# Five changes to the schedule of a network with state-space scans: places of table-switching pieces, of sums, of a copy, the share of products, and the order of directions

## The chip, the cores and the metric

The kernel runs on one core of one Trainium2 chip. The metric is the device time of one execution in microseconds (us). Most sets of executions of one kernel agree within about 0.3%; the widest, of the kernel with only the products changed, spans 0.6% (9307 to 9360). All runs told here were in the fast state, and all gave correct results. Blocks, rounds and waits are read from the one profiled run of each kernel, so differences of blocks of a few us are not clear of noise.

Engines are named as the profile names them: PE (matmuls), DVE (vector), ACT (scalar functions), POOL (GpSimd), SP (issues DMA).

## The reference, cut to what matters

Four images of 56 x 56 = 3136 tokens with 96 channels go through four layers. Layers 0 and 1 are selective scans in four directions (along rows, rows reversed, columns, columns reversed), with 192 inner channels and 16 states:

```python
def step(h, inp):
    da_t, db_t, x_t, c_t = inp
    h = da_t * h + db_t * x_t[..., None]
    y_t = jnp.einsum('bds,bs->bd', h, c_t)
    return (h, y_t)
# ... d_a = exp(softplus(dt) * a), and before and after the scans:
# norms, projections with silu, gelu, a 3x3 depthwise convolution
```

Layers 2 and 3 are a linear attention and a feed-forward block in low precision. Everything except the scans is small beside them.

## The kernel before: the parts that the change and the argument touch

The scans of one layer and image are a *block*; there are 8 (blocks 0 to 3 are layer 0, 4 to 7 layer 1). A block has 4 directions of 7 *chunks* (448 tokens), a chunk has 8 *rounds*, r = 0 to 7, which are two halves of the channels (e) by four groups of states (q). The kernel fixes the order of instructions on PE, ACT, DVE and POOL by hand:

```python
        def decay(n, g):               # ACT: da = exp(dt * a)
            ...
        def begin(n):
            b = self.spread_b(ch, q)                              # PE
            v = sp.tile([128, NG, CS + 2], F32, name="v", bufs=3)
            ahead = NQ * e + q not in (OWN_TAIL if ch.l and ch.i else OWN)
            if ahead:                                             # POOL's product
                nc.gpsimd.tensor_tensor(v[:, 2, TOKENS], ch.du[e][:, 2], ch.cb[q][:, 1], ALU.mult)
            return b, v, ahead
        ...
        for n, (ch, e, q) in enumerate(rounds):
            for g in range(2 if ahead else 3):                    # DVE's products
                nc.vector.tensor_tensor(v[:, g, TOKENS], ch.du[e][:, g], b, ALU.mult)
            nxt = begin(n + 1)
            self.prepare(ch, nexts.get(ch), r)   # next chunk: r == 2 is softplus on ACT
            yield "C", n, r                      # a slot for pieces of the rest
            if late is not None and late[2] == 0 and n > 1:
                self.keep_sums(*rounds[n - 2])   # ACT stores y (r = 1 and 5)
            for g in range(NG):
                if g == 2:
                    yield "F", n, r              # a second slot
                nc.vector.tensor_tensor_scan(...)                 # DVE
                ...
                decay(n + 1, g)                  # ACT, may start when scan g is done
                if g == 1:
                    carried(n + 1, nxt[1])       # ACT: state of the chunk before
            nc.gpsimd.tensor_tensor(hc, v, c)                     # POOL
            if late is not None:
                self.add_up(*late)               # PE: y += four * hc, one round late
            late = (ch, e, q, hc)
```

`da`, `b` and `y` each have one buffer per use in PSUM, `v` has three, `hc` two. The "rest" (loading and projections beside block 0, the middle layer beside blocks 1 to 4, fusion and attention of images 0 to 2 beside blocks 5 to 7) is cut into pieces that run in the slots. Fusion and attention of image 3 run alone after the last scan, three parts in flight and two PSUM banks for them.

## Time and profile before

| | before |
|---|---|
| time, median of three runs | 9285 us |
| first scan starts at | 121 us |
| block 0 / blocks 1 to 4, mean / blocks 5 to 7, mean | 1015 / 1083 / 1110 us |
| last scan to end | 507 us |
| mean length of rounds r = 2 in these three groups | 5.18 / 5.80 / 6.15 us |

(The prediction's 6.17 for the last of these leaves one chunk out.) Lengths of blocks and rounds in this document are read from the start times of the scans: a round lasts from its first scan to the next round's first. The prediction shows the busy times. To them belongs the list of who waited for whom (columns: engine and line, what it waited for, us in total, times, longest):

```profile
ACT Y L663 <- PE y L658: 623.0, 340, 10.0
...
DVE v L626 <- ACT v L599: 298.2, 269, 6.7
...
DVE v L612 <- PE b L535: 275.0, 185, 11.0
...
POOL hc L636 <- PE y L651: 195.5, 143, 9.6
```

The first line is `keep_sums`: ACT stood 623 us for the sums that it had to store. That is a large number on an engine that is 65% busy; whether it costs anything depends on what stands behind it in ACT's queue, which is the thread of this study. The second line is the scan that waits for the copy of the carried state, the third a product that waits for `b`, the fourth POOL, which can't overwrite `hc` until the sums have read it.

### The profile page before, as it was taken

The page shows a single profiled execution, that of the slowest core. Times are in us where ns is not written, and L with a number is a line of the kernel's source. Part 1 is how long each engine was busy: PE and PEld are TensorE (multiplying, and loading weights), DVE is VectorE, ACT ScalarE, POOL GpSimd, SP SyncE. Part 2 cuts the span into 40 slices and gives each one's busy share as a digit, 9 for nine tenths or more (in the row PEclk, how much of TensorE's full clock was granted, in tenths as well). Part 3 has the DMA queues.
Part 4 walks back from the last instruction along what each step waited for, and adds up shares of the span by engine and source line. Part 5 has one row for each costly group of instructions (what it writes and reads, how often), then busy time and mean ns, then how long its engine had stood idle before and what let it go on. Part 6 is the DMA issues. An engine that isn't in the chain of part 4 may idle for free.

```text
span 9302.9 us, 112892 instructions
## 1 busy us (share of the span) xinstructions
PE 7648.6 (82%) x30134; PEld 2655.7 (29%) x30134; DVE 7967.6 (86%) x10251; ACT 6080.1 (65%) x12093; POOL 7416.2 (80%) x3872
## 2 busy tenths in 40 slices
PE   7788787787878778887878879888898879988786
PEld 3222122222222222221222223332332223332244
DVE  5999999988998989989898989999889998999711
ACT  5777677666776667666776656666666666666523
POOL 4889888878887888878887888888888888888711
PEclk8988899888888888888898889888898889988875
DMA  5777766656666676667666676656666666666411
GB/s 154 177 177 169 172 169 162 155 138 170 168 157 147 157 172 164 155 148 172 166 162 149 154 180 154 149 148 150 176 152 155 150 154 162 157 154 153 115 33 31
DMA packets 940551, 1415.81 MB, mean 152 GB/s; under 512 B 175042, under 2 KB 926148, under 8 KB 938276
## 3 DMA queue, kind: packets, MB, share of 16 engines
q1 hardware_dynamic: 939136, 1406.79, 62.0%
q8 instruction: 238, 3.90, 0.2%
q14 instruction: 405, 3.32, 0.1%
q10 hardware_dynamic: 772, 1.80, 0.1%
HBM read 1139.85 MB, written 268.14 MB: 151 GB/s over the span
## 4 chain that ended last, share of the span: by engine, by line
PE 31%; DVE 25%; issue 12%; ACT 12%; DMA 10%; POOL 6%; SPq 3%; DVEq 0%; POOLq 0%; ACTq 0%
DVE v L626 17%; DVE v L612 7%; PE b L535 6%; PE y L651 5%; PE ps L775 4%; POOL hc L636 4%; ACT da L584 4%; DMA cb<-cd 3%; PE y L658 3%; PE pp L401 2%; DMA du<-dd 2%; PE ps L693 2%; PE ps L701 1%; SPq L485 1%; ACT L584 1%
## 5 line engine op out<-in xcount | busy, mean ns | idle before, releaser
L636 POOL TENSOR_TENSOR hc<-v,cb 128x1344 f32<-128x1344 f32 x1792 | 5155.8, 2877 | 1033.1 <-DVE v L626 571.3
L626 DVE TENSOR_TENSOR_SCAN v<-da,v 128x449 f32<-128x449 f32 (+1 forms) x5376 | 5469.6, 1071 | 362.8 <-ACT v L599 298.2
L584 ACT ACTIVATE da<-dt,na 128x448 f32<-128x448 f32 x5376 | 3358.5, 634 | 1531.4 <-DVE v L626 1477.4
L535 PE MATMUL b<-cf,sel 128*128 128x448 f32 x3584 | 2062.6, 661 | 804.5 <-DVE v L612 794.2
L612 DVE TENSOR_TENSOR v<-du,b 128x448 f32<-128x448 f32 x4172 | 2332.5, 606 | 297.3 <-PE b L535 275.0
L651 PE MATMUL y<-hc,four 128*32 128x448 f32 x14336 | 1980.0, 628 | 424.5 <-POOL hc L636 396.2
L592 POOL TENSOR_TENSOR v<-du,cb 128x448 f32<-128x448 f32 x1204 | 1378.5, 1145 | 81.1 <-DMA cb<-cd 64.9
L535 PEld LDWEIGHTS b<-cf,sel 128*128 128x128 f32 x3584 | 636.8, 212 | 2406.3 <-DVE v L612 1793.5
L651 PEld LDWEIGHTS y<-hc,four 128*32 128x32 f32 x14336 | 298.6, 114 | 1856.3 <-POOL hc L636 1104.8
L697 POOL TENSOR_TENSOR rs<-rs,power 112x4 f32<-112x4 f32 x252 | 254.3, 1010 | 685.2 <-ACT rs L696 498.5
L663 ACT COPY Y<-y 96x448 f32<-96x448 f32 x448 | 340.7, 761 | 623.8 <-PE y L658 623.0
L401 PE MATMUL pp<-U,wd 96*128 96x448 f32 x896 | 645.0, 807 | 75.1 <-DMA wd<-in_wd_dram 69.8
L775 PE MATMUL ps<-win,dg 64*64 64x220 f32 (+11 forms) x2016 | 567.3, 479 | 31.2 <-ACT w L893 30.7
L468 POOL TENSOR_TENSOR duc<-dtc,U 96x448 f32<-96x448 f32 x448 | 562.7, 1256 | 11.6 <-ACT dtc L462 11.6
L658 PE MATMUL y<-Y,ident 96*96 96x448 f32 x672 | 546.6, 902 | 0.0
L584 ACT ACT_TABLE_LOAD x385 | 494.0, 1283 | 14.4 <-DMA dt<-dd 7.5
L630 ACT COPY carry<-v 128x3 f32<-128x3 f32 x1536 | 293.6, 191 | 127.2 <-DVE v L626 123.9
L693 PEld LDWEIGHTS ps<-avg,w 96*112 96x112 f32 (+1 forms) x2240 | 315.2, 208 | 126.1 <-issue 53.2
L775 PEld LDWEIGHTS ps<-win,dg 64*64 64x64 f32 (+2 forms) x2016 | 249.6, 166 | 324.0 <-issue 255.3
L701 PE MATMUL ps<-ident,rs 112*96 112x112 f32 x2016 | 301.6, 307 | 33.3 <-POOL rs L697 31.1
L701 PEld LDWEIGHTS ps<-ident,rs 112*96 112x96 f32 x2016 | 281.5, 203 | 156.4 <-issue 77.2
L693 PE MATMUL ps<-avg,w 96*112 96x1 f32 (+1 forms) x2240 | 308.5, 255 | 20.0 <-ACT w L680 5.1
(218 smaller groups left out, 5497.3 us busy)
## 6 DMA issues: line engine op xcount, KB each, us to landing
cb<-cd SPq DMA_DIRECT2D x3584, 112.0 KB, 4.0
dt<-dd SPq DMA_DIRECT2D x1792, 168.0 KB, 4.0
du<-dd SPq DMA_DIRECT2D x1792, 168.0 KB, 3.7
dd<-dtc SPq DMA_DIRECT2D x448, 168.0 KB, 2.0
dd<-duc SPq DMA_DIRECT2D x448, 168.0 KB, 2.0
U<-u SPq DMA_DIRECT2D x64, 294.0 KB, 6.9
y<-Y SPq DMA_DIRECT2D x16, 1176.0 KB, 6.7
z<-w SPq DMA_DIRECT2D x56, 224.0 KB, 2.4
```

The costliest lines, as they stand in the source:

```text
L401: self.nc.tensor.matmul(ch.ps.rearrange("p (a b) -> p a b", b=HS), ch.par.wx[:, e], self.in_order(self.U[e], ch.orient, ch.c * CS, CS), st ...
L535: self.nc.tensor.matmul(ps, self.sel[:, q], ch.cf, start=True, stop=True)
L584: nc.scalar.activation(da[g][:, TOKENS], ch.dt[e][:, g], AF.Exp, scale=ch.par.na[:, e, q, g : g + 1])
L592: nc.gpsimd.tensor_tensor(v[:, 2, TOKENS], ch.du[e][:, 2], ch.cb[q][:, 1], ALU.mult)
L612: nc.vector.tensor_tensor(v[:, g, TOKENS], ch.du[e][:, g], b, ALU.mult)
L626: nc.vector.tensor_tensor_scan(v[:, g, way], da[g][:, way], v[:, g, way], 0.0, ALU.mult, ALU.add)
L636: nc.gpsimd.tensor_tensor(hc, v[:, :, TOKENS], ch.cb[q][:, 0].unsqueeze(1).to_broadcast([128, NG, CS]), ALU.mult)
L651: nc.tensor.matmul(self.y[32 * n : 32 * n + 32], self.four, hc[:, g], start=q == 0 or n == 3, stop=n == 3,)
L658: nc.tensor.matmul(o, w, self.in_order(a, ch.orient, ch.c * CS, CS), start=False, stop=True)
L693: nc.tensor.matmul(ps[:NT, q : q + 1], sq[:, b], avg, start=n == 0, stop=n == len(terms) - 1)
L701: nc.tensor.matmul(ps[:, b], rs[:, q : q + 1].to_broadcast([NT, C]), self.ident[:NT, :NT], start=True, stop=True)
L775: self.nc.tensor.matmul(o[:, a - r0 : e - r0, x0:x1], diag[:, tap], win[:, a + dy - lo : e + dy - lo, x0 + dx : x1 + dx], start=n == 0, st ...
```

## The change

Its intent: keep ACT from holding up the scans (table-switching pieces only at r = 0, 4, 6; the copy of carried states first), keep PE's `b` from standing behind sums that wait for POOL (sums two rounds late), take one product in eight rounds from DVE, and shorten the end (start image 3's fusion early, more parts in flight). The diff, cut to its core:

```diff
-OWN = (3, 4, 5)
-OWN_TAIL = (4, 5)
+OWN = (3, 4)
+OWN_TAIL = (3,)
-TURNS = (150, 150, 150, 150, 150, 220, 220, 220)
+TURNS = (170, 180, 160, 160, 160, 220, 220, 220)
+SWITCH = (0, 4, 6)
-ORDER = ((0, 0), (0, 1), (1, 0), (1, 1))
+ORDER = (((0, 0), (0, 1), (1, 0), (1, 1)), ((0, 1), (1, 0), (1, 1), (0, 0)))
 ...                                   # in begin(n): the copy first
+            if ch.step:
+                at = CS + 1 if ch.rev else 0
+                nc.scalar.copy(v[:, :, at : at + 1], ch.par.carry[:, e, q].unsqueeze(2))
 ...                                   # in the loop: the sums
                 nxt = begin(n + 1)
+            ended = None
+            if len(late) == 2:
+                ended = late.pop(0)
+                self.add_up(*ended)
             self.prepare(ch, nexts.get(ch), r)
             yield "C", n, r
-            if late is not None and late[2] == 0 and n > 1:
-                self.keep_sums(*rounds[n - 2])
             for g in range(NG):
                 if g == 2:
+                    if ended and ended[2] == NQ - 1:
+                        self.keep_sums(*ended[:3])
                     yield "F", n, r
 ...
-                    if g == 1:
-                        carried(n + 1, nxt[1])
 ...
-            if late is not None:
-                self.add_up(*late)
-            late = (ch, e, q, hc)
+            late.append((ch, e, q, hc))
 ...                                   # in project(): a switching piece, split
-        yield "C1"
+        yield "T1"                     # T: only where r is in SWITCH, one per slot
         (two Silu)
+        yield "F1"
         (Identity, and the next matmul)
 ...                                   # gelu, conv silu: "C" becomes "T"
 ...                                   # the end
-    alone(net.tail(3))
+    alone(rest)                        # what is left of fuse(3)
+    net.late()                         # 24 work tiles, 8 PSUM banks, 6 in flight
+    alone(net.attend(3))
```

`TURNS` is, for each block, how many of its "C" slots may start pieces, spread over the block. With the last direction of layer 1 along rows, each chunk's sums are final when it ends; they are sent out chunk by chunk, and image 3's fusion may follow them.

More of the change, by code (lines that the diff above doesn't have):

```diff
@@ L1 @@
 from contextlib import ExitStack
-from itertools import chain
+from itertools import chain, cycle
 import numpy as np
@@ L36 @@
 RANK = (12, 6)
-NW = 13
+NW, LATE_NW = 13, 24
 NWIN = 3
-OWN = (3, 4, 5)
-OWN_TAIL = (4, 5)
+OWN = (3, 4)
+OWN_TAIL = (3,)
 FULL = 4 * NCS * NE * NQ - 13
-TURNS = (150, 150, 150, 150, 150, 220, 220, 220)
-BANKS = 2
-DEPTH = 3
-ORDER = ((0, 0), (0, 1), (1, 0), (1, 1))
+TURNS = (170, 180, 160, 160, 160, 220, 220, 220)
+SWITCH = (0, 4, 6)
+BANKS, LATE_BANKS = 2, 6
+DEPTH, LATE_DEPTH = 3, 6
+ORDER = (((0, 0), (0, 1), (1, 0), (1, 1)), ((0, 1), (1, 0), (1, 1), (0, 0)))
 WD = NE * 128 + C + NE + NE * NQ * NG
@@ L167, in __init__ @@
         self.dram = pool("dram", bufs=1, space=bass.MemoryType.DRAM)
+        self.nw, self.depth, self.banks, self.ring = NW, DEPTH, BANKS, None
         self.setup()
         self.dg = None
+        self.kept = (0, 0, 0)
         self.held = self.lend = 0
+        self.switch = True
         self.U = [self.big.tile([C, L], F32, name=f"U{e}") for e in range(NE)]
         self.Y = [self.big.tile([C, L], F32, name=f"Y{e}") for e in range(NE)]
-        self.sp = pool("scan", bufs=2)
         self.wp = pool("work", bufs=2)
+        self.scan_pool = ExitStack()
+        self.sp = self.scan_pool.enter_context(tc.tile_pool(name="scan", bufs=2))
+        self.pool = pool
         d = lambda name, *shape: [self.dram.tile(list(shape), F32, name=f"{name}{i}") for i in range(NB)]
@@ L177, in __init__, with late @@
         self.ud, self.zd, self.yd, self.md = d("u", DI, L), d("z", DI, L), d("y", DI, L), d("m", DI, L)
+    def late(self):
+        self.scan_pool.close()
+        self.wp = self.pool("late", bufs=2)
+        self.nw, self.depth, self.banks = LATE_NW, LATE_DEPTH, LATE_BANKS
+        tags = (("ps", BANKS), ("da0", 1), ("da1", 1), ("da2", 1), ("pp", 1), ("b", 1), ("y", 1))
+        self.ring = cycle([t for t in tags for _ in range(t[1])])
     def ps(self):
-        return self.psum.tile([128, 512], F32, tag="ps", name="ps", bufs=BANKS)
+        tag, bufs = next(self.ring) if self.ring else ("ps", BANKS)
+        return self.psum.tile([128, 512], F32, tag=tag, name=tag, bufs=bufs)
     def w(self, rows=128):
-        return self.wp.tile([128, CW], F32, tag="w", name="w", bufs=NW)[:rows]
+        return self.wp.tile([128, CW], F32, tag="w", name="w", bufs=self.nw)[:rows]
     def par(self, group, name):
@@ L549, in scans @@
             for i in range(NB):
-                for n, (orient, rev) in enumerate(ORDER):
+                for n, (orient, rev) in enumerate(ORDER[l]):
                     for step in range(NCS):
@@ L555, in scans @@
                         ch.c = NCS - 1 - step if rev else step
-                        ch.first = n == 0 and step == 0
+                        ch.n, ch.first = n, n == 0 and step == 0
                         ch.skip = n == 0
@@ L592, in begin @@
                 nc.gpsimd.tensor_tensor(v[:, 2, TOKENS], ch.du[e][:, 2], ch.cb[q][:, 1], ALU.mult)
+            if ch.step:
+                at = CS + 1 if ch.rev else 0
+                nc.scalar.copy(v[:, :, at : at + 1], ch.par.carry[:, e, q].unsqueeze(2))
             return b, v, ahead
-        def carried(n, v):
-            ch, e, q = rounds[n]
-            at = CS + 1 if ch.rev else 0
-            if ch.step:
-                nc.scalar.copy(v[:, :, at : at + 1], ch.par.carry[:, e, q].unsqueeze(2))
         nxt = begin(0)
@@ L603, in scans @@
             decay(0, g)
-        late = None
+        late = []
         for n, (ch, e, q) in enumerate(rounds):
@@ L632, in scans @@
                     decay(n + 1, g)
-                    if g == 1:
-                        carried(n + 1, nxt[1])
             hc = sp.tile([128, NG, CS], F32, name="hc")
             nc.gpsimd.tensor_tensor(hc, v[:, :, TOKENS], ch.cb[q][:, 0].unsqueeze(1).to_broadcast([128, NG, CS]), ALU.mult)
-            if late is not None:
-                self.add_up(*late)
-            late = (ch, e, q, hc)
-        self.add_up(*late)
+            late.append((ch, e, q, hc))
+        for ended in late:
+            self.add_up(*ended)
         self.keep_sums(ch, e, q)
@@ L663, in keep_sums @@
         self.nc.scalar.copy(y, self.y[:C].rearrange("p (a b) -> p a b", b=HS))
-        if ch.last:
-            self.nc.sync.dma_start(self.yd[ch.i][C * e : C * e + C], self.Y[e])
+        if ch.n < 3:
+            return
+        s = slice(ch.c * CS, (ch.c + 1) * CS) if ch.orient == 0 else slice(0, L)
+        if ch.orient == 0 or ch.last:
+            self.nc.sync.dma_start(self.yd[ch.i][C * e : C * e + C, s], self.Y[e][:, s])
+        if e == NE - 1:
+            self.kept = (ch.l, ch.i, ch.step + 1)
     def factor(self, *x):
@@ L789, in window, with overlap @@
         return t, lo
-    def overlap(self, part, n, depth):
+    def overlap(self, part, n, depth, ready=lambda c: True):
         live, c = [], 0
         while live or c < n:
-            if self.slot == "C" and c < n and len(live) < depth:
+            if self.slot == "C" and c < n and len(live) < depth and ready(c):
                 live.append([part(c), "C0", 0])
@@ L799, in overlap @@
                 new = int(g[1][1:])
-                if g[1][0] == self.slot and sum(h[2] for h in live) - g[2] + new <= BANKS - self.lend:
+                fits = self.switch if g[1][0] == "T" else g[1][0] == self.slot
+                if fits and sum(h[2] for h in live) - g[2] + new <= self.banks - self.lend:
+                    self.switch = self.switch and g[1][0] != "T"
                     g[1], g[2] = next(g[0], None), new
@@ L827, in part @@
             yield from self.project(0, i, xr, s)
-        yield from self.overlap(part, NCW, DEPTH)
+        yield from self.overlap(part, NCW, self.depth)
     def middle(self, i):
@@ L854, in part @@
             nc.tensor.matmul(ps[0], self.w1[:, :128], xr, start=True, stop=True)
-            yield "C0"
+            yield "T0"
             g.append(self.w())
@@ L861, in part @@
                 nc.tensor.matmul(ps[m], self.w1[:, m * 128 : (m + 1) * 128], xr, start=True, stop=True)
-            yield "C0"
+            yield "T0"
             for m in (1, 2):
@@ L874, in part @@
             yield from self.project(1, i, xr, s)
-        yield from self.overlap(part, NCW, DEPTH)
+        yield from self.overlap(part, NCW, self.depth)
         if self.dg is None:
@@ L890, in convolve @@
             yield from self.conv(dga, wa, lo, (ps, c * CR, CR))
-            yield "C1"
+            yield "T0"
             t = self.w()
             nc.scalar.activation(t, ps, AF.Silu, bias=par("c128", "1conv_ba"))
+            yield "C1"
             ps = self.ps()
@@ L897, in convolve @@
             nc.sync.dma_start(self.ud[i][:128, s], t)
-            yield "C0"
+            yield "T0"
             t = self.w(64)
@@ L915, in run, with fuse @@
         yield from self.overlap(whole, 1, 1)
-    def tail(self, i):
+    def fuse(self, i):
         nc = self.nc
@@ L989, in part, with attend @@
             yield from self.gram(0, i, c, x, s)
-        yield from self.overlap(part, NCW, DEPTH)
+        yield from self.overlap(part, NCW, self.depth, lambda c: self.kept >= (1, i, c + 1))
+    def attend(self, i):
+        nc = self.nc
+        par = self.par
         for n in range(2):
@@ L1013, in ffn @@
                 yield "C1"
-                xq = self.wp.tile([C, CW], F8, name="xq", bufs=DEPTH)
+                xq = self.wp.tile([C, CW], F8, name="xq", bufs=self.depth)
                 nc.vector.tensor_tensor(xq, xs, f, ALU.mult, saturate=False)
-                h = self.wp.tile([128, 3, CW], F16, name="h", bufs=2)
+                h = self.wp.tile([128, 3, CW], F16, name="h", bufs=self.depth - 1)
                 ps = self.ps()[:, :CW]
@@ L1031, in ffn @@
                 yield "C1"
-                hq = self.wp.tile([128, 3, CW], F8, name="hq", bufs=2)
+                hq = self.wp.tile([128, 3, CW], F8, name="hq", bufs=self.depth - 1)
                 nc.vector.tensor_copy(hq, h, saturate=False)
@@ L1037, in ffn @@
                 yield "F0"
-                y = self.wp.tile([C, CW], F16, name="yq", bufs=2)
+                y = self.wp.tile([C, CW], F16, name="yq", bufs=self.depth - 1)
                 nc.scalar.copy(y, ps)
@@ L1058, in ffn @@
                 )
-            yield from self.overlap(ffn, NCW, DEPTH)
+            yield from self.overlap(ffn, NCW, self.depth)
     def gram(self, n, i, c, x, s):
         nc = self.nc
-        xr = self.wp.tile([C + 1, CW], F32, name="xra", bufs=DEPTH)
+        xr = self.wp.tile([C + 1, CW], F32, name="xra", bufs=self.depth)
         nc.vector.memset(xr[C : C + 1], 1.0)
@@ L1132, in alone @@
     def alone(stage):
-        net.slot = "C"
+        net.slot, net.switch = "C", True
         for _ in stage:
             net.slot = "CF"[net.slot == "C"]
+            net.switch = net.slot == "C"
     alone(net.load(0))
@@ L1140, in tile_net @@
         [net.load(1), net.load(2), net.load(3)], [net.middle(0)], [net.middle(1)], [net.middle(2)], [net.middle(3)],
-        [net.tail(0)], [net.tail(1)], [net.tail(2)],
+        [net.fuse(0), net.attend(0)], [net.fuse(1), net.attend(1)], [net.fuse(2), net.attend(2), net.fuse(3)],
     ]
@@ L1148, in tile_net @@
             p, u = divmod(n, rounds)
-            net.slot, net.lend = slot, int(r == 1)
+            net.slot, net.lend, net.switch = slot, int(r == 1), slot == "C" and r in SWITCH
             if slot == "C" and u == 2 and p < 8:
@@ L1152, in tile_net @@
             if u < 2 or p == 8:
+                continue
+            if p == 7 and u > FULL:
+                next(rest, None)
                 continue
@@ L1158, in tile_net @@
                 next(rest, None)
-            if u == FULL and slot == "F":
+            if u == FULL and slot == "F" and p < 7:
                 for _ in rest:
                     net.slot = "CF"[net.slot == "C"]
-    alone(net.tail(3))
+                    net.switch = net.slot == "C"
+    net.lend = 0
+    alone(rest)
+    net.late()
+    alone(net.attend(3))
 def kernel(**inputs):
```

## The prediction

> **What bounds the kernel now.** The work is 1792 rounds: 8 blocks (2 layers x 4 images) of 224 rounds, a block being 28 chunks of 8 rounds (r = 0 to 7). Each round has three scans on DVE, three exponentials on ACT, one large product `hc` on POOL, a spread `b` and four sums `y` on PE. The rest of the network is cut into pieces that are slipped in between; that of image 3 runs alone at the end. I read the busy times and costliest groups of the page first.
>
> ```profile
> PE 7648.6 (82%) x30134; PEld 2655.7 (29%) x30134; DVE 7967.6 (86%) x10251; ACT 6080.1 (65%) x12093; POOL 7416.2 (80%) x3872
> ...
> L636 POOL TENSOR_TENSOR hc<-v,cb 128x1344 f32<-128x1344 f32 x1792 | 5155.8, 2877 | 1033.1 <-DVE v L626 571.3
> L626 DVE TENSOR_TENSOR_SCAN v<-da,v 128x449 f32<-128x449 f32 (+1 forms) x5376 | 5469.6, 1071 | 362.8 <-ACT v L599 298.2
> ...
> L612 DVE TENSOR_TENSOR v<-du,b 128x448 f32<-128x448 f32 x4172 | 2332.5, 606 | 297.3 <-PE b L535 275.0
> ...
> L592 POOL TENSOR_TENSOR v<-du,cb 128x448 f32<-128x448 f32 x1204 | 1378.5, 1145 | 81.1 <-DMA cb<-cd 64.9
> ```
>
> No engine is full, but DVE and POOL are close to it in the rounds. Two idle causes make up most of DVE's waiting: scans that wait for ACT's copy of the carried state (298 us) and products that wait for PE's `b` (275 us). Then the busy time by stretch (columns: length, PE, PEld, DVE, ACT, POOL busy with counts, granted clock, DMA share, GB/s): blocks 1 to 4, blocks 5 to 7, and the end in two halves.
>
> ```profile
> 1136.00:5467.00 4331.00, 3492.86 (x13440) 1095.81 (x13440) 3871.01 (x4928) 2988.15 (x5713) 3578.92 (x1811) 0.87 0.66 160
> 5467.00:8796.00 3329.00, 2880.77 (x11926) 1045.96 (x11926) 3051.26 (x3896) 2177.07 (x4589) 2875.74 (x1539) 0.89 0.63 155
> 8796.00:9028.00 232.00, 205.07 (x729) 104.77 (x725) 24.75 (x46) 44.94 (x91) 31.92 (x29) 0.78 0.12 35
> 9028.00:9303.00 275.00, 189.47 (x642) 118.12 (x642) 41.70 (x73) 90.69 (x183) 35.44 (x35) 0.51 0.11 32
> ```
>
> The last 507 us are image 3's fusion (232) and attention (275) with DVE and POOL almost idle. In the second half PE is busy 69% at a clock of 0.51.
>
> From the start times of the scans I took each round's length. Undisturbed rounds are 4.01 us with two products on DVE (three scans at 1.00, two products at about 0.5) and 4.55 with three. So a chunk can't be under 5 x 4.01 + 3 x 4.55 = 33.7 us in blocks 0 to 4 and 6 x 4.01 + 2 x 4.55 = 33.2 in 5 to 7. Measured blocks: 1015 (block 0), 1083 on average (1 to 4), 1110 (5 to 7); 28 chunks at the floor would be 944 and 928. Rounds with r = 2 are the worst: mean 5.18, 5.80, 6.17 us in the three groups. The timeline shows why:
>
> ```profile
> 3019.50 1.28 ACT L462 ACT_TABLE_LOAD   x1
> 3020.79 0.63 ACT L462 ACTIVATE dtc<-pp,wd 96x448 f32<-96x448 f32 x1
> ...
> 3022.50 0.63 ACT L462 ACTIVATE dtc<-pp,wd 96x448 f32<-96x448 f32 x1 [1.08 <-PE pp L449]
> 3023.15 1.28 ACT L584 ACT_TABLE_LOAD   x1
> ...
> 3024.45 1.19 ACT L584 ACTIVATE da<-dt,na 128x448 f32<-128x448 f32 x2
> ...
> 3025.58 0.18 ACT L599 COPY v<-carry 128x3 f32<-128x3 f32 x1
> ...
> 3025.79 3.06 DVE L626 TENSOR_TENSOR_SCAN v<-da,v 128x449 f32<-128x449 f32 x3 [1.92 <-ACT v L599]
> ```
>
> Softplus needs another table, twice switched, and the 0.18 us copy that the scan needs stands behind two exponentials whose first was enough for the first scan. In the wait list, ACT also stands 623 us (340 times) for PE's `y` before it stores sums, and the product `hc` on POOL stands 195 us for `y`.
>
> **What the Trainium skill says.** "ScalarE: Activation LUTs", What ACT_TABLE_LOAD costs: a load is about 1283 ns, a whole switch about 2.66 us with a drain. The trace has the 1283 ns exactly, but the next activation starts 0.01 us after the load (3020.78 to 3020.79), so I count 1.28 per load and no drain. "PSUM — Partial Sum Buffer", Engine vs sequencer instructions: ACT, DVE and POOL queues are strict FIFO; the copy behind the exponentials agrees, and so moving instructions is worth something. "GPSIMD Engine Reference", Performance versus the Vector engine: a float product is 1.96 times slower on POOL at 2048 columns; here 1145 against 606 ns, 1.89. "TensorE: Matmul & The Clock Gate", Part 1: the array's clock is halved unless PE has been busy; 0.51 in the attention alone and 0.87 to 0.89 in the blocks agree.
>
> **The change part by part.**
>
> *One more product per chunk on POOL.* 8 x 28 = 224 products leave DVE (x4172 becomes 3948) and go to POOL (x1204 becomes 1428). DVE's floor falls by 224 x 0.54 = 121 us (928 and 913 per block); POOL gets 224 x 1.13 = 253 us more. POOL now needs 2.88 + 1.13 = 4.01 us in a round with its product, exactly DVE's 4.01.
>
> *Carried copy first.* It leaves the end of the exponentials for the round's start. In a round where ACT is late, the first scan then waits for one exponential, not for two and the copy: 0.63 + 0.18 = 0.8 us sooner. At r = 2 nearly every round of the three groups waits, by 0.63 (5.18 - 4.55), 1.25 and over 1.6 us; at most 0.8 of each is gained: 0.63 x 28 + 0.8 x 112 + 0.8 x 84 = 174. I take 160.
>
> *Table-switching pieces at r = 0, 4, 6.* The built program has as many table loads (98, 504, 166 in the three groups of blocks, before and after); only their rounds change. In blocks 1 to 4 a round with such a piece is longer than one without by 0.84 (r 0), 1.37 (1), 0.55 (3), 0.26 (4), 2.1 (5), 1.3 (6), 2.6 us (7), in all 140 us over 140 pieces. At r = 0, 4, 6 alone that is some 110, and the earlier copy takes most of the rest, as an exponential alone has about 3.5 us of slack against 2.57 + 0.63 for a piece. Gain about 70.
>
> *Sums two rounds late.* PE now issues the next `b` before it waits for `hc`, and ACT stores sums after two exponentials. `b` waits (275 us, of which some 64 come at image changes, where the weights' load is late) fall by perhaps 90; r = 1 and 5, where ACT stood for `y`, by some tens. Against it: `hc` of round n needs the sums of n-2, which PE now issues in round n itself, after `b`.
>
> *The end.* In the instruction order 76 of the fusion's 399 PE instructions of image 3 move into the last 20 rounds (18 were there before), since the attention of image 2 is done only by round 203. So 232 x 323/381 = 197 us, less the 9 us wait for the one large `y` transfer, about 185. The attention gets six parts in flight and eight PSUM banks for three and two. PE's 189 us of work at half clock is then the bound: 190 if the clock stays, 130 if it recovers; with start and end of two passes I take 195. The end is 380, 127 less.
>
> *Sum by block.* DVE side: block 0: 928 + 13 side work + about 25 idle = 966. Blocks 1 to 4: 928 + 18 + idle 114 (457/4) falling to 70 = 1016. Blocks 5 to 7: 913 + 88 + idle 89 falling to 70 = 1071. POOL side: busy 896, 906, 974 per block plus 32, plus its waits that aren't for DVE (103, 110, 77 now, shrinking to 50, 70, 45 as POOL arrives later): 978, 1008, 1051. Two engines so evenly loaded delay each other, so I take 980, 1022, 1075, and 12 more in the last for added fusion: 980 + 4088 + 3225 + 12 = 8305 against 8675. With 121 before the first scan and 380 at the end that is 8806 in a profiled run, some 18 less unprofiled (9285 against 9303): 8788. The gains counted one by one (121 + 160 + 70 + 100 + 127 = 578) would give 8707. I take 8770.
>
> **Rivals.** (1) POOL becomes the bound. For it: its waits (1344 us in the rounds, only 570 for DVE) are with ACT, PE and DMA and in order. If they don't shrink, the blocks are 1031, 1048, 1083, 8472 in all, and the time is about 8960. Against it: waits shrink when the waiting engine comes later. (2) PE is the real limit: 82% busy, in order, and the sums compete with `b` for the same 4 us. Then `b` waits persist and POOL's wait for `y` grows: half of the 370 gained in the rounds is lost, about 8970. (3) DVE's idle time nearly vanishes, and a warm PE clock halves the attention: blocks 960, 985, 1045 (8035 in all) and an end of 320, about 8460. (4) U of each image of layer 1 is now first read from its last quarter, as direction one is reversed: up to 10 us at four image changes, 40 us against.
>
> **Range and chances.** Between the rivals, 8 times in 10: 8590 to 8970. A time over 9099 would need the rounds to gain nothing, as the end alone gives 1.4% and DVE's lost products 1.3%: faster by over 2% 0.95, within 2% 0.04, slower 0.01.
>
> **What would show it.** Scans waiting for the copy of carried states fall from 298 to under 60 us, with part back as waits for exponentials (now 40 to about 150); mean r = 2 rounds under 5.2 us in blocks 1 to 4; ACT's wait for `y` under 250; POOL busy near 7670 and 86% of the span, its wait for DVE shrinking; after the last scan about 380 us. Wrong would be: POOL's wait for `y` over 400 us, blocks 5 to 7 not under 1100, or the attention still about 270.

## The result

The changed kernel took 9397 us (9373 to 9403, four runs) against 9286 of before: a ratio of 1.0112 with an interval of 1.0092 to 1.0133. Ratios here are the mean time of one kernel's fast runs over that of the other's of the same rounds, so they aren't quite the ratio of the medians that I quote. Within 2% counts as "same", but it is clearly slower and 427 us above the range's top, 8970. The prediction was wrong. Its profiled run was its fastest (9373), 24 us under the median; that of before (9305) was 20 above its own, so the profiled spans differ by less than the medians. (The prediction's "some 18 less unprofiled" is this scatter: the profiled run took 9304.6 us for a span of 9302.9.)

| | before | after |
|---|---|---|
| block 0 | 1015 | 1057 |
| blocks 1 to 4, mean | 1083 | 1077 |
| blocks 5 to 7, mean | 1110 | 1178 |
| last scan to end | 507 | 354 |
| r = 2 in the three groups | 5.18 / 5.80 / 6.15 | 6.46 / 6.24 / 7.58 |

The end gained 153 us, block 0 lost 42, blocks 5 to 7 lost 3 x 68, blocks 1 to 4 gained 24 in all. The sum, 42 + 204 - 24 - 153 = 69, is the difference of the two profiled spans (9371 and 9303) to 1 us. The busy times and groups of the changed kernel (lines have moved: 651 is `hc`, 643 the scan, 625 DVE's product, 608 POOL's product):

```profile
PE 7725.8 (82%) x30134; PEld 2526.8 (27%) x30134; DVE 7872.2 (84%) x10027; ACT 6081.2 (65%) x12091; POOL 7635.3 (81%) x4096
...
L651 POOL TENSOR_TENSOR hc<-v,cb 128x1344 f32<-128x1344 f32 x1792 | 5157.3, 2878 | 986.4 <-PE y L665 279.7
L643 DVE TENSOR_TENSOR_SCAN v<-da,v 128x449 f32<-128x449 f32 (+1 forms) x5376 | 5491.9, 1072 | 538.5 <-ACT da L600 446.4
...
L625 DVE TENSOR_TENSOR v<-du,b 128x448 f32<-128x448 f32 x3948 | 2212.2, 605 | 275.3 <-PE b L551 231.5
...
L608 POOL TENSOR_TENSOR v<-du,cb 128x448 f32<-128x448 f32 x1428 | 1632.5, 1143 | 94.8 <-DMA cb<-cd 94.8
```

The work moved as reckoned: 224 products less on DVE, 224 more on POOL at the same durations, POOL at 7635. No engine became full; DVE fell from 86 to 84%. What grew is the scans' idle time, 363 to 538 us, most of which is now for the exponentials (446). The same waits as before, in the changed kernel (677 is the store of sums, 611 the copy):

```profile
ACT Y L677 <- PE y L672: 524.8, 348, 5.2
DVE v L643 <- ACT da L600: 446.4, 370, 3.9
...
POOL hc L651 <- PE y L665: 279.7, 141, 11.4
...
DVE v L625 <- PE b L551: 231.5, 139, 10.5
```

The copy is no longer what scans wait for (26 us, which the full list has further down). But the store still stands 525 us for the sums. The timeline shows what stands behind it now. This is a round r = 2 of block 0, which before took 4.83 us and now took 7.04 (columns: start, us, engine, line, instruction, idle before and who ended it):

```profile
885.05 1.01 ACT L677 COPY Y<-y 96x448 f32<-96x448 f32 x1 [1.14 <-PE y L672]
885.19 3.05 DVE L643 TENSOR_TENSOR_SCAN v<-da,v 128x449 f32<-128x449 f32 x3
885.84 0.65 ACT L600 ACTIVATE da<-dt,na 128x448 f32<-128x448 f32 x1
...
886.62 1.28 ACT L478 ACT_TABLE_LOAD   x1
...
890.27 1.28 ACT L600 ACT_TABLE_LOAD   x1
...
891.57 1.19 ACT L600 ACTIVATE da<-dt,na 128x448 f32<-128x448 f32 x2
892.24 1.09 DVE L643 TENSOR_TENSOR_SCAN v<-da,v 128x449 f32<-128x449 f32 x1 [2.42 <-ACT da L600]
```

ACT waits 1.14 us for the sums and stores them for 1.0 us; only then come the third exponential and softplus with its two table loads, and then the exponentials of the next round, for which the scan waits 2.42 us. The softplus load starts 1.43 us after the round's first scan (886.62 - 885.19). In the round that the prediction shows of before, it started 0.25 us after it (3019.50; that scan began at 3019.25). In the next chunk of block 0 before (the first of a direction), the store waits much the same, 1.10 us, but stands some 3 us earlier against r = 2, at the start of r = 1:

```profile
892.57 3.04 DVE L626 TENSOR_TENSOR_SCAN v<-da,v 128x448 f32<-128x448 f32 x3
...
893.47 0.99 ACT L663 COPY Y<-y 96x448 f32<-96x448 f32 x1 [1.10 <-PE y L658]
...
896.39 1.28 ACT L462 ACT_TABLE_LOAD   x1
896.57 3.04 DVE L626 TENSOR_TENSOR_SCAN v<-da,v 128x448 f32<-128x448 f32 x3
```

The first scan is that of r = 1, the second that of r = 2; between the store and softplus ACT has caught up. As medians over all chunks of the three groups, the load started at -0.18, -0.03 and 0.40 us before, and at 1.51, 1.21 and 1.74 after. At r = 5 the other store of a chunk stands in the same way before the pieces of r = 6: those rounds grew from 4.07 to 5.07 us in block 0 and from 4.47 to 4.91 in blocks 1 to 4.

The end, in two halves as in the prediction (fusion and attention; columns as there):

```profile
9016.80:9200.00 183.20, 160.29 (x629) 85.35 (x629) 23.33 (x48) 35.64 (x73) 27.14 (x25) 0.83 0.15 45
9200.00:9371.00 171.00, 129.65 (x615) 85.19 (x614) 39.39 (x64) 85.04 (x182) 36.11 (x35) 0.70 0.14 38
```

The attention's first instruction starts at 9196.6, so the cut is good to some 4 us. With six parts in flight and eight PSUM banks PE is busy 76% of the attention at a clock of 0.70; before, with three and two, it was 69% at 0.51.

### The profile page after: what moved, and what is told of

Its sections match the earlier page's. It is cut to its first block, busy times and chain, and to the rows that moved or that the text cites. A ratio compares the mean times of both kernels' runs of the same rounds, so it can differ in the third digit from the quotient of the medians.

```text
span 9371.1 us, 113059 instructions
## 1 busy us (share of the span) xinstructions
PE 7725.8 (82%) x30134; PEld 2526.8 (27%) x30134; DVE 7872.2 (84%) x10027; ACT 6081.2 (65%) x12091; POOL 7635.3 (81%) x4096
## 5 line engine op out<-in xcount | busy, mean ns | idle before, releaser
L551 PE MATMUL b<-cf,sel 128*128 128x448 f32 x3584 | 2086.6, 668 | 1240.1 <-DVE v L625 1230.1
L625 DVE TENSOR_TENSOR v<-du,b 128x448 f32<-128x448 f32 x3948 | 2212.2, 605 | 275.3 <-PE b L551 231.5
L665 PE MATMUL y<-hc,four 128*32 128x448 f32 x14336 | 2048.5, 648 | 41.9 <-POOL hc L651 32.6
L608 POOL TENSOR_TENSOR v<-du,cb 128x448 f32<-128x448 f32 x1428 | 1632.5, 1143 | 94.8 <-DMA cb<-cd 94.8
L600 ACT ACT_TABLE_LOAD x385 | 494.0, 1283 | 16.5 <-DMA dd<-duc 9.6
L611 ACT COPY v<-carry 128x3 f32<-128x3 f32 x1536 | 281.0, 183 | 111.9 <-POOL hc L651 110.6
L713 PEld LDWEIGHTS ps<-avg,w 96*112 96x112 f32 (+2 forms) x2152 | 274.6, 194 | 149.3 <-issue 42.0
L465 PE MATMUL pp<-cf,wd 12*96 12x448 f32 (+1 forms) x528 | 281.9, 615 | 19.4 <-ACT dtc L478 19.2
L713 PE MATMUL ps<-avg,w 96*112 96x1 f32 (+2 forms) x2152 | 284.8, 249 | 8.6 <-ACT w L700 5.7
```

What stands on the lines that cost most here:

```text
L551: self.nc.tensor.matmul(ps, self.sel[:, q], ch.cf, start=True, stop=True)
L600: nc.scalar.activation(da[g][:, TOKENS], ch.dt[e][:, g], AF.Exp, scale=ch.par.na[:, e, q, g : g + 1])
L665: nc.tensor.matmul(self.y[32 * n : 32 * n + 32], self.four, hc[:, g], start=q == 0 or n == 3, stop=n == 3,)
L713: nc.tensor.matmul(ps[:NT, q : q + 1], sq[:, b], avg, start=n == 0, stop=n == len(terms) - 1)
```

## The experiments

They ran in four sets, on three chips (numbers 11, 13 and 15), and each set had the kernel before beside it. So kernels of different sets are compared by their ratios to before; a difference of ratios times 9290 gives us.

My theory after the first look (S): the sums behind `b`, and their store between the second and third exponential, make ACT late right in front of softplus. Its rivals: POOL has too much to do (P); the copy, now first, makes ACT stand for POOL (C); the pieces crowd at r = 0, 4, 6 (T).

### One part undone in the changed kernel

**Sums as before.**

```diff
-            ended = None
-            if len(late) == 2: ended = late.pop(0); self.add_up(*ended)
+            if late and late[0][2] == 0 and n > 1: self.keep_sums(*rounds[n - 2])
-                    if ended and ended[2] == NQ - 1: self.keep_sums(*ended[:3])
+            if late: self.add_up(*late.pop())
             late.append((ch, e, q, hc))
```

> The changed kernel with sums and their storing where they were before (one round late, store at the start of r = 1 and 5); all else changed. Theory S (ACT's store of sums now stands, waiting for PE's y, between the second and third exponential of r = 1 and 5, right ahead of softplus at r = 2 and of the pieces at r = 6): rounds r = 2 fall from 6.45, 6.26 and 7.7 us (blocks 0, 1-4, 5-7) to under 5.2, 5.4, 6.2; block 0 under 1010 us, blocks 1-4 about 1040, blocks 5-7 about 1120, time about 9000. Rival P (POOL, which got 224 more products, is what holds the rounds): blocks 5-7 stay over 1150 and the time over 9250.

Measured 9156 us (9144 to 9163), ratio to before 0.9846 (0.9826 to 0.9867): the late sums cost (1.0112 - 0.9846) x 9290 = 247 us here. Rounds r = 2 fell to 5.35, 5.50 and 6.21. Blocks were 1045, 1054 and 1138: every group gained, but not as far as expected, and blocks 5 to 7 were still 28 us above those of before. Rounds r = 6 fell to 4.25 and 4.24 in blocks 0 to 4. So S holds, and is not all.

**Products shared as before.**

```diff
-OWN = (3, 4)
-OWN_TAIL = (3,)
+OWN = (3, 4, 5)
+OWN_TAIL = (4, 5)
```

> The changed kernel with DVE's and POOL's products shared as before (OWN 3,4,5; tail 4,5). Theory S: r = 2 of block 0 stays over 6 us, blocks 0 to 4 change by under 15 us each; blocks 5-7 gain less than 30 each; time 9300 to 9400. Rival P: blocks 5-7 fall from 1178 to about 1110, blocks 1-4 by 20 or more, time under 9150.

Measured 9466 us, ratio 1.0181; slower, which neither theory had. Blocks 1064, 1094, 1180. In the changed kernel the new share is worth (1.0181 - 1.0112) x 9290 = 64 us, nearly all in blocks 0 to 4; rival P falls as the main cause.

**Copy as before.**

```diff
+                    if g == 1:
+                        carried(n + 1, nxt[1])     # and not in begin()
```

> The changed kernel with the copy of carried states back behind the second exponential. Theory S, and the prediction's reckoning of the copy: r = 2 gets longer by up to 0.8 us (block 0 about 7.2), time about 9500. Rival C (the copy, now first, makes ACT stand for POOL's hc, 111 us in the waits, and that is what delays softplus): r = 2 gets shorter and the time falls to 9300 or less.

Measured 9514 us, ratio 1.0231: r = 2 of block 0 rose to 7.06. The copy first is worth 111 us in this company, and rival C falls.

**Pieces as before** (any round but r = 2, old turns; the split in the projection stays).

```diff
-TURNS = (170, 180, 160, 160, 160, 220, 220, 220)
+TURNS = (150, 150, 150, 150, 150, 220, 220, 220)
-                fits = self.switch if g[1][0] == "T" else g[1][0] == self.slot
+                fits = (self.slot == "C") if g[1][0] == "T" else g[1][0] == self.slot
```

> The changed kernel with table-switching pieces in any round but r = 2 and the turns of before. Theory S: pieces again in r = 1 and 5 add to the late ACT there; blocks 1-4 change by under 25 us either way, blocks 5-7 (which have no such pieces) by nothing (under 10); time 9350 to 9480. Rival T (three rounds of eight crowd pieces at r = 0 and 6, where the trace shows 4.8 and 4.9 us): blocks 1-4 fall by 30 each, time about 9270.

Measured 9349 us, ratio 1.0055. In the two profiles, blocks differ by 7, -3 and -6 us: little, and rival T's 30 us in blocks 1 to 4 aren't there. The time fell by some 50 us, the profiles by 24; which rounds gave it, I can't say.

### What remained after the sums

**Sums as before, and blocks 5 to 7 shared as before.**

```diff
 (sums as before)
-OWN_TAIL = (3,)
+OWN_TAIL = (4, 5)
```

> The changed kernel with sums as before, and in blocks 5-7 the products shared as before (4,5 on DVE); blocks 0-4 keep the new share. Beside the run with sums as before (9156; blocks 5-7 at 1138 on average against 1110 before the change). Theory P' (in blocks 5-7 POOL now has its product in the two rounds r = 3 and 4 in which it also has 1.25 us of step size products, and loses it in r = 2, where softplus makes everyone wait anyway): blocks 5-7 fall to about 1100, time about 9040. Rival O (the other order of directions, or the split of the stage, slows blocks 5-7): they stay at 1130 or more, time 9130 to 9200.

Measured 9110 us, ratio 0.9781 (0.9762 to 0.9801), 60 us better than with the new share (0.9846). Blocks 5 to 7 fell from 1138 to 1121: less than P' wanted, and still 11 over before. My reading: POOL makes the product of a round during the round before, so in the new share r = 2 is the one round without POOL's product, though softplus leaves POOL time there, while r = 3 and 4 have `hc`, a product and a step-size product of 1.25 us each, 2.88 + 1.14 + 1.25 = 5.3 us. That this is why is argued, not shown. By rounds, r = 3 and 4 got longer (4.76 to 5.26 and 4.60 to 5.00: DVE's products of r = 4 and 5 are made there), and the gain is at r = 2 (6.21 to 5.75), r = 5 (5.29 to 4.80) and r = 7 (5.46 to 5.20). So DVE's product was not free in front of r = 3's scans, as P' had it; what fits is that POOL's lateness from r = 3 and 4 showed in the rounds after.

**Only the end changed** (the kernel before with the new order of directions, early fusion, and the last attention).

```diff
 (kernel before, with ORDER, fuse/attend, late() and chunkwise output of the change)
```

> The kernel before with only the end changed: last direction of layer 1 along rows, fusion of image 3 begun in the last rounds, six parts in flight in the last attention; sums, copy, products and pieces as before. If the parts add, blocks are as before (1015, 1083, 1110) and the end is about 355 instead of 507: time about 9140 (0.984). Rival O: blocks 5-7 lengthen by 20 us or more each, time 9200 or more.

Measured 9220 us, ratio 0.9912. The end is 353 us, 154 shorter, but blocks 5 to 7 are 1127 on average, 17 longer (9, 14 and 29). By direction, the first two directions of each of these blocks got 4 to 10 us longer, and the chunk before the last of blocks 5 and 6, in which the next image's U (the input of its scans) is awaited, 6 to 8 us: rival O in kind, if under its 20 us. Block 7 has besides the start of image 3's fusion: its last direction got 11 us longer.

**Sums and pieces as before.**

```diff
 (sums as before, TURNS and pieces as before)
-        yield "F1"                     # the projection's piece in one again
```

> The changed kernel with sums and table-switching pieces (with turns, and the projection's piece in one again) as before; copy first, products and end as changed. Theory F (the projection's piece is split and its second half, on ACT in the F slot, is what the next matmul on PE waits for, 3 us in front of the next b): block 0 falls from 1045 to about 985 and blocks 1-4 from 1054 to about 1035, PE's wait for ACT in the projection under 12 us (44 now), time about 9010. Rival: pieces at r = 0, 4, 6 are worth their gain, and blocks 1-4 get longer, by 10 us or more each; time 9150 or more.

Measured 9184 us, ratio 0.9871. Both sides have a part: block 0 fell from 1045 to 1007, as theory F said, and blocks 1 to 4 rose from 1054 to 1069, as the rival said. The kernel with sums as before shows the split's harm in its timeline, at a chunk of block 0:

```profile
296.19 0.63 ACT L751 ACTIVATE w<-ps,inb 64x448 f32<-64x448 f32 x1
...
296.87 1.86 PE L753 MATMUL ps<-w,in 96*128 96x448 f32 x2 [3.23 <-ACT w L751]
...
303.55 1.15 DVE L625 TENSOR_TENSOR v<-du,b 128x448 f32<-128x448 f32 x2 [4.49 <-PE b L551]
```

The second half of the piece stands behind two exponentials on ACT. The next matmul wants its PSUM bank, PE waits 3.23 us; sums and `b` stand behind it in PE's order, and DVE waits 4.49 us for that `b`. What of it is the split and what the rounds of the pieces, this run does not part; the run without the split below does.

**Sums early, store late.** It parts the two halves of the late sums.

```diff
 (add_up one round late as before)
-                    if ended and ended[2] == NQ - 1: self.keep_sums(*ended[:3])
+                    if late and late[0][2] == 0 and n > 1: self.keep_sums(*rounds[n - 2])
```

> The changed kernel with the sums' matmuls one round late as before, but their store on ACT where the change has it (between the second and third exponential). It parts theory S in two. If it is the store's place and length (1.0 us ahead of softplus), r = 2 of block 0 is about 6.2 and the time over 9300. If it is the wait for y, because PE now issues the sums after b, r = 2 of block 0 falls to about 5.5 and the time is about 9150 or less, as with all undone (9156).

Measured 9121 us, ratio 0.9798 (0.9781 to 0.9814). It is the lateness of the sums, not the store's place: r = 2 of block 0 is 5.26, and the softplus load starts 0.19 us after the scan in block 0 (1.51 in the changed kernel). With the sums ready in time the store is even better placed there than at the round's start (9156; the ratios' intervals, to 0.9814 and from 0.9826, don't meet).

### Parts alone, and mixtures

**Only the sums, in the kernel before.**

```diff
 (kernel before, with the change's lines for late, add_up and keep_sums)
```

> The kernel before with only the sums two rounds late. Theory S: r = 2 lengthens in every group (block 0 from 5.18 to 6.3 or more), blocks lengthen by 12 to 40 us, time about 9430 to 9500 (ratio 1.015 to 1.025), ACT's copies of carried states then hold up the scans over 400 us. The prediction's step (about 100 us gained) would give 9200.

Measured 9685 us (9675 to 9696), ratio 1.0415 (1.0401 to 1.0429): 386 us slower, more than S expected. Blocks 1061, 1116, 1177; r = 2 at 6.49, 6.88, 7.61. Two waits grew:

```profile
DVE v L630 <- ACT v L599: 444.0, 250, 9.3
POOL hc L640 <- PE y L654: 379.7, 268, 9.9
...
DVE v L630 <- ACT da L584: 213.6, 198, 4.3
```

Scans wait for ACT 658 us in these two lines (298 + 40 before), and POOL waits 380 us for `y` (195 before), since PE now reads the `hc` of round n-2 in round n, just before POOL wants to overwrite it. These are the two waits of the cause by themselves: ACT's late exponentials and copies, and POOL's wait for `y`.

**Only the products, in the kernel before.**

```diff
-OWN = (3, 4, 5)
-OWN_TAIL = (4, 5)
+OWN = (3, 4)
+OWN_TAIL = (3,)
```

> The kernel before with only the share of products changed (OWN 3,4; tail 3). The prediction took 121 us off DVE's floor and said that POOL's extra 253 us would be mostly hidden: 9180. Theory P' (DVE's product was free where ACT held the round up, POOL's is not): blocks 0 to 4 shorten by 10 or less each, blocks 5-7 lengthen by 15 or more each, time 9290 to 9340.

Measured 9337 us, ratio 1.0037 (1.0022 to 1.0052): no gain at all. Blocks 1010, 1086, 1129.

```profile
PE y L651 <- POOL hc L636: 479.5, 498, 7.2
...
DVE v L612 <- PE b L535: 393.3, 269, 13.3
```

POOL's longer rounds make `hc` late, PE's sums stand for it 480 us (396 before), and `b` behind them is late for DVE: 393 against 275 us. What DVE no longer has to do, it waits for. This is read from the list of waits; no run parts it.

**Only the copy, in the kernel before.**

```diff
 (kernel before, with the copy moved into begin() as in the change)
```

> The kernel before with only the copy of carried states first. The prediction's term is 160 us: about 9140, r = 2 of blocks 1-4 from 5.80 to about 5.1, waits of scans for the copy from 298 to under 60 us. Rival (the wait moves: PE's b and the exponentials are late by then as well): r = 2 stays over 5.5, time 9220 or more.

Measured 9219 us, ratio 0.9917 (0.99 to 0.9933): 77 us. r = 2 of blocks 1 to 4 fell from 5.80 to 5.49. Scans no longer wait for the copy, but 229 us for exponentials (40 before).

**The end and the pieces** (projection in one), against only the end.

```diff
 (only the end changed, plus SWITCH, T slots and TURNS; no F1)
```

> The kernel with only the end changed (9220), and the table-switching pieces with their turns at r = 0, 4, 6, the projection's piece in one. The prediction's term is 70 us, all in blocks 0 to 4: 9150. Rival (a piece costs about the same wherever the copy waits behind it, 0.84 and 1.3 us at r = 0 and 6): blocks 1-4 shorten by under 8 us each, time 9190 or more.

Measured 9141 us, ratio 0.9840 against 0.9912: (0.9912 - 0.9840) x 9290 = 67 us, all in blocks 1 to 4 (1085 to 1066), while block 0 lost 6. Here the copy is still late.

**Sums early, store late, projection in one, blocks 5 to 7 shared as before.**

```diff
 (sums early, store late)
-OWN_TAIL = (3,)
+OWN_TAIL = (4, 5)
-        yield "F1"
```

> The changed kernel with the sums one round late, the store where the change has it, the projection's piece in one, products of blocks 5-7 shared as before. From the single steps: 9121 less 50 (products of blocks 5-7) less 37 (theory F: block 0 falls from 1038 to about 1003) less some in blocks 1-4: about 9030 (0.970). Rival to F (turns or rounds of the pieces, not the split, cost block 0 its 37 us): block 0 stays over 1025, time about 9070.

Measured 9029 us (9004 to 9041), ratio 0.9706 (0.969 to 0.9723), as added up. Blocks 1008, 1045, 1123. It beats both kernels. The same place as above in its timeline, block 0 (ACT alone):

```profile
854.58 0.98 ACT L675 COPY Y<-y 96x448 f32<-96x448 f32 x1
855.34 0.64 ACT L600 ACTIVATE da<-dt,na 128x448 f32<-128x448 f32 x1
...
856.12 1.28 ACT L478 ACT_TABLE_LOAD   x1
```

The store does not wait. Theory F's 37 us in block 0 came as 30 (1038 to 1008).

**Mixed sums:** as the last, but only the sums that a store waits for (q = 3) early, the others behind `b`.

```diff
+            if late and late[0][3] is None: ended = late.pop(0)
+            elif len(late) == 2: self.add_up(*late.pop(0))
 ...
             late.append((ch, e, q, hc))
+            if len(late) == 2 and late[0][2] == NQ - 1:
+                self.add_up(*late[0]); late[0] = (*late[0][:3], None)
```

> The changed kernel with only the sums that a store waits for (q = 3) issued one round late, ahead of b, and the others two rounds late behind b; store where the change has it; the projection's piece in one; products of blocks 5-7 shared as before. If the late sums are good in themselves and only the wait of the store in front of softplus was bad, this is better than the same kernel with all sums one round late (run beside it, expected about 9050): b waits on DVE under 300 us, r = 2 of block 0 under 5.3, time about 8980. Rival L (sums behind b are of no use at all, since POOL then waits for y): 9050 or more.

Measured 9096 us, ratio 0.9783, 72 us worse than with all sums early. `b` waits fell as wanted (363 to 300 us), and still it lost: rival L. POOL's wait for `y` (155 to 194) and the scans' for exponentials (185 to 256) rose. Rounds r = 2 of block 0 fell to 4.92 us (5.25 with all sums early), so without the store's wait the late sums do not hurt r = 2; their 72 us of harm are spread over other rounds. Late sums are of no use here even where no store waits for them; which of the two waits did it is not settled.

**Products undone everywhere**, beside the best.

```diff
-OWN = (3, 4)
+OWN = (3, 4, 5)
```

> As c3_late_store_unsplit (9029), but the products shared as in the kernel before everywhere (3,4,5; 4,5). If DVE's lighter load is worth what its products take (140 products of 0.54 in blocks 0-4), the time rises by about 75 to 9105. If POOL's longer path takes it all back, as with the products alone (9337 against 9300), the time stays within 20 of 9029 or falls.

Measured 9047 us, ratio 0.9737 (0.9717 to 0.9756), against 0.9706: by these the share of blocks 0 to 4 is worth (0.9737 - 0.9706) x 9290 = 29 us, where its floor promised 140 x 0.54 = 76. The two intervals touch, and by the medians it is 18: the second expectation (within 20) is nearer than the first.

**Order of directions undone**, beside the best.

```diff
-ORDER = (..., ((0, 1), (1, 0), (1, 1), (0, 0)))
+ORDER = (..., ((0, 0), (0, 1), (1, 0), (1, 1)))
-            self.kept = (ch.l, ch.i, ch.step + 1)
+            self.kept = (ch.l, ch.i, NCS if ch.last else 0)
```

> As c3_late_store_unsplit (9029), but directions of layer 1 in the order of before, so that the fusion of image 3 can't begin before the last scan. Theory U (the new order reads U last quarter first and puts a direction along columns, with its slow strided matmuls, beside the fusion's convolution): blocks 5-7 fall from 1123 to about 1107 each, the end lengthens from 353 to about 395, time about 9020. Rival (the order is not it): blocks 5-7 stay at 1118 or more, time about 9070.

Measured 9041 us, ratio 0.9730 (0.9715 to 0.9745). Blocks 5 to 7 fell from 1123 to 1109, and the end grew from 353 to 416. The order, with the early fusion that it allows, takes 3 x 15 = 44 us in the blocks of what it gives at the end, 63; theory U holds on the place, though not on the time (9020): the order is worth (0.9730 - 0.9706) x 9290 = 22 us net, and the intervals touch. That U's last quarter and the column direction beside the convolution are its two halves is argued from where the time appears, not tried one by one.

## Why the prediction was wrong, point by point

| term of the prediction's sum | predicted | alone | in the changed kernel (against the part undone) |
|---|---|---|---|
| products to POOL | -121, mostly kept | +34 (ratio 1.0037) | -64 |
| copy first | -160 | -77 (0.9917) | -111 |
| pieces at r = 0, 4, 6 | -70 | -67 (0.9912 to 0.9840), unsplit | about +50, with split |
| sums two rounds late | -100 | +386 (1.0415) | +247 |
| the end | -127 | -82 (0.9912) | not tried |

**The step that failed** is "Sums two rounds late". It said that waits for `b` would fall by perhaps 90 and that r = 1 and 5 "where ACT stood for `y`" would gain "some tens". In themselves both came true in part: `b` waits fell from 275 to 163 us in the kernel with only this part, and r = 1 of blocks 1 to 4 fell from 4.91 to 4.49 (of blocks 5 to 7 it did not, 4.56 to 4.61). The prediction did say that "ACT stores sums after two exponentials", and put no cost on it. What it overlooked is that the store and its wait did not vanish (623 us before, 525 in the changed kernel). They moved from the start of r = 1, where ACT had a whole round to catch up, to the end of r = 1, directly in front of softplus, which with its two table loads held ACT for 4.9 us in the round shown (886.62 to 891.55). Softplus then started 1.5 us after the round's first scan in block 0, and r = 2 grew from 5.18 to 6.46 us. The prediction had measured how late ACT may be at r = 2, had listed the 623 us of the store's wait, and did not put the two side by side. The second rival ("the sums compete with `b` for the same 4 us") named POOL's wait for `y`, which did double in the kernel with the sums alone; but its figure, 8970, was far too mild. How the 386 us divide between the two waits is not measured; in the company of the mixed kernel the late sums cost 72 us where the store hardly waits.

**Copy first.** Mechanism right (scans wait 26 us for it), size off by half: with the copy moved, the first exponential itself is late, which I had allowed for, and at r = 2 only 0.31 of the hoped 0.8 us came in blocks 1 to 4.

**Products.** The arithmetic of the move was exact (POOL 7635 predicted near 7670, DVE 224 products fewer). Wrong was to take the floor's 121 us for time. By the waits, PE's sums hand POOL's lateness on to `b`, so DVE waited instead; alone the part lost 34 us. In blocks 5 to 7 the choice of the round is bad as well: 60 us in the run that undid it there.

**Pieces.** Right in size, 67 for 70, once the projection is in one, but in part by luck. The prediction had counted how much longer the rounds with a piece are, 140 us in all, and expected 110 at r = 0, 4, 6, and most of the rest from the earlier copy. The 67 us came in a kernel with the late copy, and the same count there still gives 134 us (2.13 at r = 0, 0.25 at r = 4, 0.85 at r = 6); the gain shows in the rounds r = 1 and 5 (4.81 to 4.35 and 4.63 to 4.30 in blocks 1 to 4). The split, which I had not looked at, cost block 0 some 30 us.

**The end.** Fusion 183 us for the predicted 185; attention 171 for 195, with the clock at 0.70 for 0.51 and PE busy 130 us for 189; together 354 for 380. Not foreseen in size was the price in blocks 5 to 7, 17 us each on average; the fourth rival had named U's last quarter with up to 40 us in all.

**The signs.** Of what was to show it wrong, one came: blocks 5 to 7 not under 1100. Of what was to show it right, the copy (26), POOL's busy time (though 81% of the span for 86), its shorter wait for DVE (571 to 235) and the end came; ACT's wait for `y` under 250 (525), exponentials at about 150 (446) and r = 2 under 5.2 (6.24) did not. The chance of 0.95 for faster rested on "a time over 9099 would need the rounds to gain nothing". They lost.

The single parts add to 34 - 77 - 67 + 386 - 82 = 194 us, the kernel lost 104, with the split's harm in it, which the sum leaves out: parts depend on each other. In the changed kernel the moved products are useful (-64 for +34) and the early copy more so (-111 for -77); which other part makes them so was not tried. One thing more stays open: the mean granted clock differs too (0.845 with the sums alone against 0.867 before, 0.885 in the best against 0.871 in the changed kernel), and no run shows whether it took part or only followed.

## What to carry to other kernels

A wait that is moved in an engine's order may do more harm in its new place, as the store's did here: before moving an instruction, ask what will stand behind it, and above all whether that is the longest job of its engine. Time taken off one engine's busy sum is worth only what the waits for the other engines let through; here 121 us off DVE gave nothing alone. When several schedule changes come in one step, measure each alone and each undone: one part of five, worth +386 us alone, hid the others, which together beat the kernel before by 2.9% (with the split and the share of blocks 5 to 7 undone too).

## What the Trainium skill lacked or had wrong

- "ScalarE: Activation LUTs", What ACT_TABLE_LOAD costs: the load's 1283 ns is exact in both kernels. The drain of about 1380 ns that the page adds to a switch doesn't appear as a gap before the next activation: it starts 0.01 us after the load's end (3019.50 + 1.28 = 3020.78, next 3020.79). Nor is it a gap before the load: ACT's idle time before all 225 loads of softplus is 4.1 us in the kernel before.
- "TensorE: Matmul & The Clock Gate", Part 1: agrees in kind. It lacks a figure for a chain of small dependent matmuls; here PE busy 69% had a mean clock of 0.51, and 76% one of 0.70, in the same stage with three parts in flight and two PSUM banks, and with six and eight.
- "PSUM — Partial Sum Buffer", Engine vs sequencer instructions, says that ACT, DVE and POOL queues are strict FIFO, and PE's matmuls start and complete in program order. I know of no page that says how far a wait travels by this: the sums placed behind one more `b` in PE's order, with their store in front of softplus, made ACT, then the exponentials, then DVE's scans late, and POOL's wait for `y` double: 386 us of 9300 with the same work.
